# PSUM tiles from a pool in the unplanned part of a long-convolution decoder layer

## The chip, the cores and the metric

The kernel runs on one core of a Trainium2 chip. The metric is the device time of one execution in microseconds, as the median of several runs. A profile is one execution; its span runs from the first to the last instruction on the core, and the time of that execution is a little longer than its span.

## What is computed

One decoder layer with post-normalisation, on x of 4 x 1024 x 256 in float32:

```python
x = layernorm(x + longconv(x))         # projection to 3*256, depthwise conv of 3 taps,
                                       # two gated convolutions over all 1024 positions (by FFT)
x = layernorm(x + cross_attention(x, ctx))   # 16 heads, 64 context rows per batch
x = layernorm(x + ffn(x))              # gate/up/down of 1024, ternary weights, 8-bit activations
```

The filters of the two convolutions are themselves computed: `h = sin(10*(pe @ w1.T + b1)) @ w2.T + b2`, times a decay, plus a bias.

## The kernel before

The convolution is done with DFT matrices in place of an FFT. The channels are split into eight units: batch `b` (four) and half `dh` (two) of the 256 channels. Even and odd positions are kept apart, so that one transform of 1024 positions becomes small f32 matmuls against the tables `fw` (forward) and `gi_` (inverse).

Before the units comes the filter stage. `filter_basis` (L473) multiplies `pe` by `w1`, prepares the argument of the sine on VectorE, and lets ScalarE compute eight decay tiles (exponentials, into `q1_t`) and the sine. `stage_j(0)` issues the projections of unit 0 between the two halves of the filter work. `filters` (L489) then makes eight products with `w2` (`hp`), multiplies each by its decay on VectorE, and transforms the result with eight tiles of four `fw` matmuls each (`ha`); ScalarE copies one half of each `ha` tile out and VectorE forms sum and difference into `hf`.

Each unit goes through these stages:

- `stage_j` (L578): three projections of x (`project`, L533): four matmuls into one PSUM tile, which ScalarE reads four times: two halves into `xc` or `x1c`, and two shifted copies into `tap` tiles. GpSimd then issues two DMAs that add the taps onto `xc`, one after the other. There are two pairs of taps, so the third projection's taps wait until the first pair has been added.
- `stage_tv` and `stage_tx`: eight TensorE transposes of `xc` each, and one ScalarE copy into `vt` or `x0t`.
- `stage_f` (L599): the forward transform, 16 matmuls in two PSUM tiles; ScalarE copies a half, VectorE adds and subtracts.
- `stage_p` (L624): the product with the filter, on VectorE alone, into `q`.
- `stage_i0` (L669): the inverse transform, 16 matmuls into one PSUM tile. Parts 0, 1, 2 (12 matmuls) are issued ahead of the next unit's `stage_tv`, and part 3 behind it. `stage_i1` is the second convolution's inverse.
- `stage_o`: output projection, residual and layernorm.

The loop at L793 runs over units 0 to 6 and interleaves the stages of neighbouring units. Two things set the order. Up to unit 5 every call goes to the framework at once (line L61 in the profile); the framework's scheduler puts the instructions of an engine in order and may move one ahead of another where their data and their PSUM allow it. From unit 6 on (`if u == NU - 2`, L796) the calls are held back (`nc.hold`), the kernel's own planner (`plan`, L232) puts all held steps in order by estimated costs, and that order is pinned (line L82 in the profile, the call in `Engines.go`).

PSUM is one tile `ps_t` of 128 x 4096 f32, all eight banks (L412). A ring (`r_ps`) hands out four slots of 1024 columns, two banks each, strictly in turn. The framework tracks reads and writes of `ps_t` by bank. After the loop `space_of["rest"]` is set to the third slot, and the other slots go to attention and feed-forward (`big`, `small`).

Of the kernel before, what the change touches and what calls it, by code (L numbers as in the profile page):

```python
# [8 lines left out]
FP = mybir.dt.float32  # L9
# [5 lines left out]
PSUM = bass.MemoryType.PSUM  # L15

P = 128
# [266 lines left out]
def decoder_kernel(  # L284
# [63 lines left out]
    def split_biases():  # L348
        rest = spare[1][:, 0:6]
        nc.sync.dma_start(rest, rows.rearrange("r d -> (r d)").rearrange("(p c) -> p c", p=P))  # L350
        nc.gpsimd.memset(brow, 0.0)
        for q in range(3):
            part = spare[1][:, 8 + 8 * q : 16 + 8 * q].bitcast(BF)[:, 0:6]
            nc.vector.tensor_copy(part, rest)
            nc.sync.dma_start(
                brow[32 * q : 32 * q + 1].rearrange("o r d -> o (r d)").rearrange("o (p c) -> o p c", p=P), part
            )
            if q < 2:
                tt_(rest, rest, part, ALU.subtract)
# [49 lines left out]
    mw = const.tile([P, 3], FP, name="mw")  # L409
    rw = const.tile([P, 3], FP, name="rw")  # L410

    ps_t = ctx.enter_context(tc.tile_pool(name="ps", bufs=1, space=PSUM)).tile([P, 4096], FP, name="ps_t")  # L412
    r_ps = Ring(*(ps_t[:, 1024 * i : 1024 * i + 1024] for i in range(4)))
    space_of = {}

    def big1(name):
        return space_of["rest"] if space_of else r_ps()

    if True:
        taps = [tap_t[2 * i : 2 * i + 2] for i in range(NTAP)]  # L420
# [157 lines left out]
        def stage_j(u, *parts):  # L578

            b, dh = units[u]  # L580
            s = st_[u]
            for k in parts or range(3):
                name, ring, ct = (("vc", r_xc, 4), ("xc", r_xc, 0), ("x1", r_x1c, 2))[k]
                s[name] = ring()
                project(u, ct + dh, s[name])
                if k == 2 and dh == 1 and b + 1 < B:
                    load_x(b + 1)

        def stage_tv(u):
            s = st_[u]  # L590
            s["v"] = r_vt()
            turned(u, s["vc"], s["v"], "v")

        def stage_tx(u):
            s = st_[u]
            s["x0"] = r_x0t()
            turned(u, s["xc"], s["x0"], "x")

        def stage_f(u, n):  # L599

            s = st_[u]
            v = s["v"].rearrange("p (t d) -> p t d", t=8)
            vf = r_vf().rearrange("p (c s f) -> p c s f", c=2, s=2)
            s["vf"] = vf
            for cs in range(2):
                ps = big1(f"f{u}_{n}_{cs}")
                for par in range(2):
                    for kt in range(2):
                        o = par * 512 + kt * 256
                        m = (2 * cs + kt) * P  # L610
                        for mt in range(2):
                            mm(
                                ps[:, o : o + 256],
                                fw[:, 2 * par + mt, m : m + P],
                                v[:, 4 * par + 2 * mt : 4 * par + 2 * mt + 2, :],
                                start=mt == 0,
                                stop=mt == 1,
                            )
                vo = vo_t
                nc.scalar.copy(vo, ps[:, 512:1024])  # L620
                tt_(vf[:, cs, 0, :], ps[:, 0:512], vo, ALU.add)
                tt_(vf[:, cs, 1, :], ps[:, 0:512], vo, ALU.subtract)
# [46 lines left out]
        def stage_i0(u, *parts):  # L669

            s = st_[u]
            y = s["q", 0][1]
            if not parts or parts[0] == 0:
                s["i0"] = big1(f"i0_{u}")
            ps = s["i0"]
            for i in parts or range(4):
                par, mt = i // 2, i % 2
                o = i * 256
                for m in range(4):
                    mm(  # L680
                        ps[:, o : o + 256],
                        gi_[:, m, par * 256 + mt * P : par * 256 + mt * P + P],
                        y[:, par, m // 2, (m % 2) * 256 : (m % 2) * 256 + 256],
                        start=m == 0,
                        stop=m == 3,
                    )
            if not parts or parts[-1] == 3:
                s["v"] = r_vt()
                tt_(s["v"], ps, s["x0"], ALU.mult)

        def stage_i1(u):

            s = st_[u]
            b, dh = units[u]
            if dh == 0:
                v2s[b] = v2_t.rearrange("p (h l) -> p h l", h=2)
            y = s["q", 1][1]
            ps = big1(f"i1_{u}")
            for par in range(2):
                for j in range(2):  # L700
                    o = (2 * par + j) * 256
                    for m in range(4):
                        c = (m % 2) * 256 + j * P
                        mm(
                            ps[:, o : o + 256],
                            y[:, par, m // 2, c : c + P],
                            gi_[:, m, par * 256 : par * 256 + 256],
                            start=m == 0,
                            stop=m == 3,
                        )  # L710
            tt_(v2s[b][:, dh, :], ps, s["x1"], ALU.mult)

        def stage_o(b):

            for g in range(2):
                r = x1all[2 * b + g]
                nc.sync.dma_start(r, tokens(x, 2 * b + g))
                ps = big1(f"o{b}_{g}")
                for t in range(4):
                    c = (4 * g + t) * P  # L720
                    o = ps[:, t * D : t * D + D]
                    mm(o, ones16, brow[:, 0, :], start=True, stop=False)
                    for kt in range(2):
                        mm(o, v2s[b][:, kt, c : c + P], w_out_sb[:, kt, :], start=False, stop=kt == 1)
                rf = r.rearrange("p t d -> p (t d)")
                tt_(rf, ps, rf, ALU.add)
                layernorm(r, r, f"a{b}_{g}")
# [49 lines left out]
        def weights(u, place):  # L777
            for step, i in w_plan.get((u, place), ()):
                ternary(step, i)

        def move(i, dst):
            nc.sync.dma_start(dst, w_res[i])
# [10 lines left out]
        for u in range(NU - 1):  # L793
            if u == 1:
                split_biases()
            if u == NU - 2:  # L796

                nc.hold()
                nc.at = -40
            stage_p(u, 0, 0)  # L800
            weights(u, "p")
            nc.at += 1
            if u >= 2:
                stage_i1(u - 2)
            stage_p(u, 0, 1)
            nc.at += 1
            stage_j(u + 1, 0)
            nc.at += 1
            if u >= 1:
                stage_f(u - 1, 1)  # L810
            nc.at += 1
            stage_j(u + 1, 1, 2)
            nc.at += 1
            if u >= 1:
                stage_p(u - 1, 1, 0)
            nc.at += 1
            stage_i0(u, 0, 1, 2)
            weights(u, "i")
            nc.at += 1
            stage_tv(u + 1)  # L820
            nc.at += 1
            stage_i0(u, 3)
            weights(u, "t")
            nc.at += 1
            stage_f(u + 1, 0)
            nc.at += 1
            stage_tx(u + 1)
            nc.at += 1
            if u >= 1:
                stage_p(u - 1, 1, 1)  # L830
            nc.at += 1
            if u >= 2 and units[u - 2][1] == 1:
                stage_o(units[u - 2][0])

    u = NU - 1
    rest = [
        lambda: stage_p(u, 0, 0),
        lambda: stage_i1(u - 2),
        lambda: stage_p(u, 0, 1),
        lambda: stage_f(u - 1, 1),  # L840
        lambda: (move(0, hfree[1][:, 0:1024]), move(1, hfree[1][:, 1024:2048])),
        lambda: stage_p(u - 1, 1, 0),
        lambda: (stage_i0(u), stage_f(u, 1)),
        lambda: stage_p(u - 1, 1, 1),
# [14 lines left out]
    def small(name, dtype=FP):  # L859
        v = ps_t[:, 3072:3584] if name[0] in "akp" else ps_t[:, 3584:4096]  # L860
        return v if dtype == FP else v.bitcast(dtype)
# [32 lines left out]
    for dt in range(2):  # L894
        ps = small(f"k{dt}")
# [7 lines left out]
    for b in range(B):  # L903
        ps = small(f"v{b}")
# [272 lines left out]
                nc.at, nc.stage = i, "rest"  # L1177
                rest.pop(0)()

    space_of["rest"] = ps_t[:, 2048:3072]  # L1180
    nc.stage = "att_q"
    att_q(0)
    remains(2, 0)
    i, h = 0, 0
# [123 lines left out]
```

## Time and profile before

| | us |
|---|---|
| median of 3 runs | 764.66 (764.33 to 764.86) |
| the profiled execution | 765.34 |
| its span | 763.5 |
| TensorE matmuls busy | 710.0 (93%) |
| VectorE busy | 651.4 (85%) |
| ScalarE busy | 373.4 (49%) |
| GpSimd busy | 150.3 (20%) |
| mean granted TensorE clock | 0.974 of full |

How to read the rows: a row of the timeline starts with the start in us from the span's start, then the time it took, engine, source line, operation, output and inputs by the program's names, shapes, and the number of like instructions merged into it; in brackets stands the idle time of that engine before it and what ended it. PE is TensorE, DVE VectorE, ACT ScalarE, POOL GpSimd, SP SyncE. Tile numbers are left out of names, and all PSUM is `ps_t`. An f32 matmul makes two records and a transpose one. In the page, each digit of a line of 40 slices is a tenth of busy share, and PEclk is the TensorE clock that was granted. In rows by stretches of time the columns are the stretch, its length, busy time and number of instructions of PE, PE's weight loads, DVE, ACT and POOL, the granted clock, the busy share of the DMA engines and GB/s.

### The profile page before, as it was taken

What the parts mean: (1) busy time and instruction counts of PE and PEld (TensorE: products, weight loads), DVE (VectorE), ACT (ScalarE), POOL (GpSimd) and SP (SyncE); (2) the same over time, 40 slices, a digit from 0 to 9 for tenths busy, and PEclk for the clock granted to TensorE, in tenths of its full rate; (3) what the DMA queues carried; (4) which work ended last, traced back from release to release, by engine and by line L of the source; (5) the groups of instructions that cost most, each with busy time, mean ns of one, the idle gap of its engine ahead of it and who ended that gap; (6) DMA issues with size and microseconds to landing.
All of it is one profiled execution on the core that took longest, in us unless ns stands there. A gap on an engine that the chain in (4) does not pass through costs nothing. (4 is left out here: it accounts for less than half of the span.)

```text
span 763.5 us, 9645 instructions
## 1 busy us (share of the span) xinstructions
PE 710.0 (93%) x3606; PEld 511.0 (67%) x3606; DVE 651.4 (85%) x1189; ACT 373.4 (49%) x430; POOL 150.3 (20%) x214
## 2 busy tenths in 40 slices
PE   5899599999999999998999999999999999999863
PEld 1346286868687787876788787757676767767631
DVE  3446719999999999599979997989999999999984
ACT  2712516245361525224332213687778777868631
POOL 1210211111121112112000220122222322322322
PEclk9989989999999999999999999999999999999985
DMA  8572553537470644609601000012131322121232
GB/s 282 124 133 110 121 100 65 101 56 142 69 159 16 138 83 82 112 6 177 180 10 55 1 1 1 1 36 49 43 56 36 63 43 63 29 48 41 49 70 48
DMA packets 65140, 57.29 MB, mean 75 GB/s; under 512 B 38500, under 2 KB 49252, under 8 KB 65094
## 3 DMA queue, kind: packets, MB, share of 16 engines
q0 software_dynamic: 13056, 25.17, 19.3%
q1 hardware_dynamic: 47612, 27.84, 14.2%
q10 hardware_dynamic: 4426, 3.68, 1.7%
q8 instruction: 28, 0.46, 0.2%
q14 instruction: 18, 0.15, 0.1%
HBM read 17.34 MB, written 4.19 MB: 28 GB/s over the span
## 5 line engine op out<-in xcount | busy, mean ns | idle before, releaser
L82 PE MATMUL ps_t<-hf 128*128 128x512 bf16 (+1 forms) x512 | 100.3, 334 | 16.6 <-DMA hf<-vf 7.3
L82 PEld LDWEIGHTS <-hf 128*128 128x128 bf16 (+1 forms) x512 | 48.2, 100 | 57.7 <-issue 23.2
L61 PE MATMUL ps_t<-vt,fw 128*128 128x256 f32 x384 | 85.2, 380 | 0.9 <-ACT vt L61 0.6
L61 PEld LDWEIGHTS ps_t<-vt,fw 128*128 128x128 f32 x384 | 72.8, 190 | 13.5 <-issue 2.4
L61 PE MATMUL ps_t<-xt,w_in 128*128 128x512 f32 x168 | 76.4, 607 | 5.1 <-DMA w_in<-in_w_inT 5.1
L61 POOL DMA_DIRECT2D xc<-tap x28 | 33.9, 1245 | 207.1 <-ACT tap L61 133.5
L82 POOL TENSOR_TENSOR small_t<-small_t,mhalf 128x1 f32<-128x1 f32 x64 | 36.4, 574 | 157.6 <-DVE small_t L82 155.7
L82 PEld LDWEIGHTS ps_t<-hf,vt 128*128 128x128 f32 x512 | 61.0, 192 | 8.8 <-DVE small_t L82 3.1
L82 PE MATMUL ps_t<-hf,vt 128*128 128x34 f32 x512 | 61.9, 275 | 1.9 <-DVE xt L82 0.7
L61 PEld LDWEIGHTS ps_t<-xt,w_in 128*128 128x128 f32 x168 | 32.5, 195 | 43.1 <-issue 41.9
L61 ACT ACTIVATE tap<-ps_t,tbias,pv 128x1024 f32<-128x1024 f32 x42 | 48.6, 1210 | 11.4 <-DMA xc<-tap 11.4
L61 DVE TENSOR_TENSOR q<-q 128x1024 f32<-128x1024 f32 x44 | 53.0, 1218 | 0.4
L61 DVE TENSOR_TENSOR q<-vf,hf 128x1024 f32<-128x1024 f32 (+1 forms) x33 | 51.8, 1575 | 0.6
L61 ACT ACTIVATE xc<-ps_t,cbias,pv 128x512 f32<-128x512 f32 x28 | 21.5, 778 | 61.7 <-PE ps_t L61 61.7
L82 DVE SCALAR_TENSOR_TENSOR q<-ps_t,small_t,q 128x1024 f32<-128x1024 f32 x32 | 40.9, 1278 | 7.6 <-PE ps_t L82 4.6
L82 ACT ACTIVATE vf<-q,chalf,small_t 128x1024 f32<-128x1024 f32 x32 | 39.5, 1236 | 15.8 <-POOL small_t L82 8.1
L82 ACT ACTIVATE tap<-tap 128x1024 f32<-128x1024 f32 x32 | 33.8, 1056 | 25.6 <-DVE tap L82 25.4
L61 ACT COPY vo<-ps_t 128x512 f32<-128x512 f32 x24 | 14.0, 585 | 64.1 <-PE ps_t L61 47.4
L61 PE MATMUL ps_t<-q,gi__123 128*128 128x256 f32 x192 | 45.4, 393 | 0.0
L82 ACT ACT_TABLE_LOAD x34 | 43.6, 1283 | 2.2 <-PE ps_t L82 1.6
L82 ACT ACTIVATE q<-ps_t,small_t 128x1024 f32<-128x1024 f32 x32 | 35.6, 1113 | 17.5 <-PE ps_t L82 14.4
L61 DVE TENSOR_TENSOR vf<-ps_t,vo 128x512 f32<-128x512 f32 x48 | 31.1, 683 | 14.7 <-ACT vo L61 14.7
(149 smaller groups left out, 1493.4 us busy)
## 6 DMA issues: line engine op xcount, KB each, us to landing
xc<-tap POOLq DMA_DIRECT2D x32, 512.0 KB, 5.1
x1c<-tap POOLq DMA_DIRECT2D x16, 512.0 KB, 7.1
xt<-in_xT SPq DMA_DIRECT2D x8, 512.0 KB, 6.3
x1sp<-in_x SPq DMA_DIRECT2D x8, 512.0 KB, 4.6
out_y<-v SPq DMA_DIRECT2D x32, 128.0 KB, 1.7
hf<-x1sp SPq DMA_DIRECT2D x3, 512.0 KB, 2.9
fw<-in_dftf SPq DMA_DIRECT2D x1, 1024.0 KB, 14.0
gi__123<-in_dfti SPq DMA_DIRECT2D x1, 1024.0 KB, 10.7
```

What stands on the lines that cost most here:

```text
L61: return f(*a, **k)
L82: pin(steps[i].f(*steps[i].a, **steps[i].k))
```

## The change

The one PSUM tile of the whole kernel is split in time. Up to the planned part, each request for PSUM makes a tile of its own from a pool with four slots of 1024 columns; the framework assigns a slot that is free at that point of its schedule, and releases it when the last reader of that tile is done. Where the planned part begins the pool is closed, and a second pool is opened with one tile `ps_t` over all of PSUM; from there a ring of four slots serves as before, starting at its first slot. The function `big1` picks between the two. After the loop the third slot is wrapped in a ring of one, since `big1` now calls what it finds.

```diff
-    ps_t = ctx.enter_context(tc.tile_pool(name="ps", bufs=1, space=PSUM)).tile([P, 4096], FP, name="ps_t")
-    r_ps = Ring(*(ps_t[:, 1024 * i : 1024 * i + 1024] for i in range(4)))
+    psa = tc.tile_pool(name="psa", bufs=4, space=PSUM)
+    psa_p = psa.__enter__()
+
     space_of = {}
 
     def big1(name):
-        return space_of["rest"] if space_of else r_ps()
+        return space_of["rest"]() if space_of else psa_p.tile([P, 1024], FP, tag="big", name=name)
...
             if u == NU - 2:
 
+                psa.__exit__(None, None, None)
+                psb = ctx.enter_context(tc.tile_pool(name="psb", bufs=1, space=PSUM))
+                ps_t = psb.tile([P, 4096], FP, name="ps_t")
+                space_of["rest"] = Ring(*(ps_t[:, 1024 * i : 1024 * i + 1024] for i in range(4)))
                 nc.hold()
                 nc.at = -40
...
-    space_of["rest"] = ps_t[:, 2048:3072]
+    space_of["rest"] = Ring(ps_t[:, 2048:3072])
```

## The prediction

> **What bounds the kernel now.** I read the page's slices first, to see where TensorE is not full; then TensorE's and ScalarE's rows of the first 110 us in order of time; then the granted clock in 10 us stretches; then the place where the first pool closes.
>
> ```profile
> span 763.5 us, 9645 instructions
> ...
> PE   5899599999999999998999999999999999999863
> ...
>
> ```
>
> A slice is 19.1 us. TensorE is full except in slices 0, 1, 4 (76 to 95 us), 18 (344 to 363) and the end. From 107 us on it hardly waits: in 120 to 322 the waits view gives it 0.3 us in all, and in 366 to 480 0.7 us. So a microsecond won before 107 us moves everything after it. Rows of TensorE:
>
> ```profile
> 33.79 1.12 PE L61 MATMUL ps_t<-vf,x1sp 65*128 65x512 f32 x2
> 34.75 1.02 PE L61 MATMUL ps_t<-x1sp,fw 128*128 128x512 f32 x2
> 39.59 2.08 PE L61 MATMUL ps_t<-vf,x1sp 65*128 65x512 f32 x2 [3.82 <-ACT tap L61]
> 41.46 1.92 PE L61 MATMUL ps_t<-x1sp,fw 128*128 128x512 f32 x2
> 43.17 1.55 PE L61 MATMUL ps_t<-vf,x1sp 65*128 65x512 f32 x2
> ...
> 67.73 1.54 PE L61 MATMUL ps_t<-ident,xc 128*128 128x128 f32 x12
> 69.87 7.17 PE L61 MATMUL ps_t<-vt,fw 128*128 128x256 f32 x32 [0.60 <-ACT vt L61]
> 76.88 0.60 PE L61 MATMUL ps_t<-ident,xc 128*128 128x128 f32 x4
> 77.32 10.46 PE L61 MATMUL ps_t<-xt,w_in 128*128 128x512 f32 x24
> 96.19 1.94 PE L61 MATMUL ps_t<-ident,xc 128*128 128x128 f32 x8 [8.40 <-DMA xc<-tap]
> 97.92 9.22 PE L61 MATMUL ps_t<-q,gi__123 128*128 128x256 f32 x32
> ```
>
> Two stalls, 3.82 and 8.40 us, and slow matmuls behind each (an f32 matmul is two records, a transpose one). ScalarE's rows name the cause of the first:
>
> ```profile
> 16.24 0.78 ACT L61 ACTIVATE xc<-ps_t,cbias,pv 128x512 f32<-128x512 f32 x1 [8.83 <-PE ps_t L61]
> 16.92 4.99 ACT L61 ACTIVATE q<-vf,pv 128x512 f32<-128x512 f32 x8
> ...
> 38.33 1.21 ACT L61 ACTIVATE tap<-ps_t,tbias,pv 128x1024 f32<-128x1024 f32 x1 [4.60 <-DMA xc<-tap]
> ```
>
> A read of a projection stands ahead of eight exponentials that need no TensorE, so these, the table load and the sine run to 24.3, and the taps start only then. The last tap waits for an accumulating DMA and holds its PSUM slot to 39.54; ring order gives that slot to the seventh w2 product. Granted clock:
>
> ```profile
> 40.00:50.00 10.00, 10.00 (x19) 4.16 (x19) 5.34 (x8) 1.17 (x2) 2.40 (x2) 0.79 1.05 203
> 90.00:100.00 10.00, 3.81 (x13) 3.46 (x14) 2.02 (x2) 2.22 (x2) 3.45 (x3) 0.60 1.03 217
> ```
>
> [...] here the pair onto xc takes 5.0 and 7.4, so I use the trace's. [...]
>
> **Part 1, the filter stage.** The built order of the changed kernel differs. (a) ScalarE does exponentials, table load and sine before it reads the projection: from 7.4, 4.99 + 1.28, sine after VectorE's argument (14.57), done near 15.7. The first projection ends at 16.8, so its reads and taps end near 20.6 (27.1 before); the first accumulate goes out near 19.8 (26.35), the pair is home near 30, and the last tap is done near 31 (39.54). (b) Slots come free, not in turn: all eight w2 products go first, on whichever slot is free, then the 32 fw matmuls. None waits for the last tap before the third fw tile. TensorE's work is equal, 8 and 32.
>
> w2 products still start at 25.05, after the projections. The gate becomes VectorE: the second product waits for the first's read and ends at 27.87; the first fw tile waits for the read of the sixth, nine VectorE instructions on at about 0.69: 27.9 + 6.2 = 34.1. Thirty-two fw at (67.73 - 44.56)/27 = 0.858 take 27.5, so the transposes start at 61.7, not 67.73: -6.0, of which 3.6 is the stall less the new gaps and 2.4 the slow clock (39.59 to 44.56 for three matmuls worth 2.57). VectorE, then the end of ScalarE's vt copy, move along; the f stage starts at 63.8. Here four transposes of x no longer hide in the 0.60 wait but follow f: +0.44. Projections start at 71.7 and end at 82.2: -5.6.
>
> **Part 2, the first inverse transform.** Before, the v transposes, waiting for the accumulate until 96.19, stood ahead of all 16 inverse matmuls (97.92). In the changed order 12 of the 16 stand ahead of them, in a slot of their own. They need only VectorE's q: its last three rows start at 88.40 and end at 92.02, the second near 90.8; with -6.0 that is 84.8, a stall of 2.6 instead of 8.40. Warm, a stage of 16 takes 6.90 (322.95 to 329.85), so 12 take 5.2; a 2.71 us stall at 355 cost 1.8 extra (16 f matmuls in 8.70, not 6.90). I take it slow: done at 91.8. The accumulate, home at 96.05 before, moves by 5.6 to 90.4: hidden. Eight transposes 0.87, four inverse matmuls 1.73: f starts at 94.4 instead of 106.98: **-12.6**. Warm it would be -13.8.
>
> **Part 3, units 1 to 5.** A tile is now released whole, by its last reader, where a bank was before: TensorE's first write waits for ScalarE and VectorE together. Behind that wait stands all of TensorE. But a slot is reused some three tiles on, 3.4 to 7 us of TensorE work; ScalarE's waits in 120 to 322 show none on a DMA. Cost 0, at most 0.5 a unit. Nineteen more semaphore instructions on TensorE's queue: matmul spacing around the present ones (0.21 or 0.43) is undisturbed; 0, at most 1 in all.
>
> **Part 4, where the pool closes.** The new tile covers all of PSUM, so its first writer waits for the last readers of the old pool.
>
> ```profile
> 322.08 1.03 PE L61 MATMUL ps_t<-w_out_sb,v 128*128 128x256 f32 x4
> 322.95 7.07 PE L82 MATMUL ps_t<-gi__123,q 128*128 128x256 f32 x32
> ...
> 324.84 1.22 DVE L61 TENSOR_TENSOR x1sp<-ps_t,x1sp 128x1024 f32<-128x1024 f32 x1
> ...
> 357.71 8.86 PE L82 MATMUL ps_t<-vt,fw 128*128 128x256 f32 x32 [2.71 <-ACT vt L82]
> ```
>
> The planned inverse transform would start at 326.1, not 322.95: 3.2 us, and about 1.8 of slow clock: +5.0. VectorE isn't behind it: it reads that result at 337.81, ready at 335.0. Then comes the 2.71 us stall at 355 with its 1.8: 4.5 us of cover. The vt copy moves only with ScalarE's queue (projection reads about +1.6, and context loads issued behind them), and the second xc1 accumulate, home at 366.08 for the transposes at 366.41, moves as much. I take +1.2 of the 5.0; bounds -0.5 and 5.0. The plan's early order moves a few key projections and transposes by about a microsecond with no wait: 0. From there on the order is that of before.
>
> **Sum.** -12.6 + 1.2 = -11.4. The profiled execution is 765.34 us, 763.5 of it span: 753.9. The median shown is 764.66, 0.7 lower, so **753.3 us**.
>
> **Rivals.** *B, the pool's close is paid in full:* if ScalarE's reads and the DMA pair also slip by the whole 5.0, -12.6 + 5.0 gives 757.1. For: the pair ahead of 366 has only 0.3 us to spare. Against: it is issued behind VectorE-bound work.
> *C, the first accumulates don't come home earlier:* they run at a DMA share of 1.03 beside the x load. If the v transposes still start at 96.1, f starts at 96.1 + 0.87 + 1.73 = 98.7: -8.3 + 1.2 gives 757.6.
> *D, slower:* whole-tile release puts the second tap of a projection in TensorE's way in every unit. Price: one blocked tap, 6.25 us in the trace (before 96.13), of which some 3 would show. It decides from 11.4/6 = 1.9 us a unit; at 3.0 the time is 764.7 - 11.4 + 18 = 771. Against: in the unit at 114.76 taps end at 121.4, some 5 us before the slot is wanted.
> *E, no change:* the order differs, but something at a fixed time takes the gain back. No load in 107 to 340 is such a bound; 764.7.
>
> **How the numbers follow.** Forecast 0.64 (its own range 750.8 to 756), B 0.15, C 0.11, D 0.06, E 0.04. Low end: -13.8 and a close at zero. High end: C with 1.4 of other waits. 750.5 to 759 leaves out D, E and a little. A difference of 0.2% (1.5 us) is about what a measurement of this kernel can tell. Faster 0.90, same 0.04, slower 0.06.
>
> **What would show it.** The transposes of unit 0 near 61.7; ScalarE's eight exponentials before its first projection read; 12 inverse matmuls ahead of the v transposes of unit 1 and f near 94; no TensorE wait over 0.5 us between there and 310; a TensorE wait of some 3 us on VectorE's x1sp near 313 and less than 1 us where 2.71 stood. A wait on a tap in each unit, or v transposes of unit 1 held past 95 by the DMA, would prove me wrong.

## The result, and the profile after

| | before | after |
|---|---|---|
| median, first measurement | 764.50 us (764.01 to 764.86, 4 runs) | 754.53 us (752.98 to 759.92, 4 runs) |
| ratio after/before, 95% interval | | 0.9883 (0.9833 to 0.9932) |
| the profiled execution, and its span | 765.34, 763.5 | 752.98, 751.2 |
| TensorE matmuls busy | 710.0 | 705.3 |
| mean granted TensorE clock | 0.974 | 0.986 |

The kernel is 1.2% faster; 753.3 us was forecast for the median. Two further measurements of the changed kernel on other chips gave 0.9867 (0.984 to 0.9895) and 0.9872 (0.9841 to 0.9903). By the medians measured beside each other the gain was 10.0, 9.4 and 11.2 us; 11.4 was forecast. The single times of the changed kernel lie further apart (752.98 to 759.92 us) than the first four of before did. The kernel before scatters as widely when it is measured more often (761.3 to 770.1 us in 27 runs), so this is no effect of the change; what it consists of comes under the first experiment.

First the page of the changed kernel: its span and TensorE's line of 40 slices.

```profile
span 751.2 us, 9662 instructions
...
PE   5999899999999999899999999999999999999862
```

Between the first slice and the last three, all are full but two: 75 to 94 us and 300 to 319 us, an 8 each. Next TensorE's rows in order of time. The PSUM tiles have names of their own now: `trv` of the v transposes, `pj` of projections, `i` of the inverse, `o` of the output projection.

```profile
61.61 1.04 PE L61 MATMUL trv<-ident,xc 128*128 128x128 f32 x8
...
71.63 10.47 PE L61 MATMUL pj<-xt,w_in 128*128 128x512 f32 x24
84.81 7.03 PE L61 MATMUL i<-q,gi__122 128*128 128x256 f32 x24 [2.72 <-DVE q L61]
91.69 1.04 PE L61 MATMUL trv<-ident,xc 128*128 128x128 f32 x8
```

Compared with the starts of before, in brackets, the v transposes of unit 0 are at 61.61 (67.73) and the projections at 71.63 (77.32). The stall of 8.40 us on `xc<-tap` is gone; 12 inverse matmuls start at 84.81 after 2.72 us on VectorE's q, and the v transposes come behind them without a wait. f of unit 1 follows at 94.29, where before it was:

```profile
106.98 7.07 PE L61 MATMUL ps_t<-vt,fw 128*128 128x256 f32 x32
```

ScalarE's rows show why the filter stage is shorter:

```profile
7.53 5.01 ACT L61 ACTIVATE q<-vf,pv 128x512 f32<-128x512 f32 x8
...
33.52 1.21 ACT L61 ACTIVATE tap<-pj,tbias,pv 128x1024 f32<-128x1024 f32 x1 [5.36 <-DMA xc<-tap]
```

The exponentials run at 7.53 instead of 16.92, ahead of the first projection read, which now comes at 18.36 with its taps right behind it. The last tap is done at 34.73 instead of 39.54. The stretch that had a clock of 0.60 before:

```profile
90.00:100.00 10.00, 10.00 (x52) 8.87 (x51) 2.63 (x4) 2.81 (x3) 2.40 (x2) 1.00 0.97 168
```

It is full and at full clock, and so is the one from 40 to 50 us, which had 0.79. Last, the place where the pool closes, TensorE and VectorE:

```profile
313.18 8.83 PE L82 MATMUL ps_t<-gi__122,q 128*128 128x256 f32 x32 [3.10 <-DVE x1sp L61]
...
346.83 7.07 PE L82 MATMUL ps_t<-vt,fw 128*128 128x256 f32 x32
353.74 1.04 PE L82 MATMUL ps_t<-ident,xc 128*128 128x128 f32 x8
```

```profile
311.82 1.22 DVE L61 TENSOR_TENSOR x1sp<-o,x1sp 128x1024 f32<-128x1024 f32 x1
```

The first planned inverse waits 3.10 us for VectorE's residual add, and its 16 matmuls take 8.83 instead of 7.07 (the clock from 310 to 320 us is 0.83). But f at 346.83 has no wait, where before 2.71 us stood with 8.86 behind it. The x transposes of unit 7 come next, at 353.74; before they stood here:

```profile
366.41 1.04 PE L82 MATMUL ps_t<-ident,xc 128*128 128x128 f32 x8
```

The stretch from the end of the output projection to these transposes is 43.46 us before (322.95 to 366.41). In the changed kernel the last group of the output projection starts at 309.05; before, the next group came 0.87 after such a start (322.08 to 322.95), which puts its end at 309.92 and makes the stretch 43.82 us. The difference of 0.36 is that of the two waits, each with what its matmuls lost: 3.10 + 1.76 in place of 2.71 + 1.79.

### The profile page after: what moved, and what is told of

Same layout as the page of the kernel before. It is cut to its first block, busy times and chain, and to the rows that moved or that the text cites. A ratio compares the mean times of both kernels' runs of the same rounds, so it can differ in the third digit from the quotient of the medians.

```text
span 751.2 us, 9662 instructions
## 1 busy us (share of the span) xinstructions
PE 705.3 (94%) x3606; PEld 508.9 (68%) x3606; DVE 650.5 (87%) x1189; ACT 372.7 (50%) x430; POOL 151.1 (20%) x214
## 5 line engine op out<-in xcount | busy, mean ns | idle before, releaser
L61 PE MATMUL f<-vt,fw 128*128 128x256 f32 x384 | 84.9, 379 | 1.1 <-ACT vt L61 1.1
L61 PEld LDWEIGHTS f<-vt,fw 128*128 128x128 f32 x384 | 72.9, 190 | 13.3 <-issue 2.4
L61 PE MATMUL pj<-xt,w_in 128*128 128x512 f32 x168 | 75.8, 604 | 5.7 <-DMA w_in<-in_w_inT 5.7
L61 PEld LDWEIGHTS pj<-xt,w_in 128*128 128x128 f32 x168 | 32.3, 194 | 43.3 <-issue 42.6
L61 ACT ACTIVATE tap<-pj,tbias,pv 128x1024 f32<-128x1024 f32 x42 | 48.8, 1218 | 11.4 <-DMA xc<-tap 11.3
L61 ACT ACTIVATE xc<-pj,cbias,pv 128x512 f32<-128x512 f32 x28 | 20.3, 777 | 59.3 <-PE pj L61 59.3
L61 PE MATMUL i<-q,gi__122 128*128 128x256 f32 x192 | 45.1, 390 | 2.7 <-DVE q L61 2.7
L82 ACT ACTIVATE tap<-tap 128x1024 f32<-128x1024 f32 x32 | 33.8, 1056 | 26.9 <-DVE tap L82 26.8
L61 PEld LDWEIGHTS i<-q,gi__122 128*128 128x128 f32 x192 | 37.1, 196 | 10.7 <-DVE q L61 3.5
L61 DVE TENSOR_TENSOR vf<-f,vo 128x512 f32<-128x512 f32 x48 | 31.1, 683 | 14.4 <-ACT vo L61 14.4
```

Of the source, the lines that this page charges most:

```text
L61: return f(*a, **k)
L82: pin(steps[i].f(*steps[i].a, **steps[i].k))
```

## The experiments

In what follows the transposes at 353.74 of the changed kernel are x transposes of unit 7; those at 344.23 are its v transposes. Where an expectation speaks of v transposes of unit 7 at 353.7, the former are meant.

Theory: the change works through the order of instructions in two early places, and its close puts one wait in the place of another. Rivals: that it needs slots handed out of turn; that the close costs several microseconds which a better version would save.

### The changed kernel again

> The changed kernel once more, to see how far its four times (752.98 to 759.92 us, the kernel before 764.01 to 764.86) are its own. Theory 'the gain is 12.4 us and the rest is scatter': the profiled execution again has unit 0's v transposes at 61.6, f of unit 1 at 94.3, the 3.1 us wait at 313 and f of the planned part at 346.8, each within 0.3 us, and the median lies 11 to 12.5 us below before. Rival 'the new order is sensitive to when the transfers come home': one of these places moves by more than 1 us, and the long executions are long there.

> The changed kernel a third time, beside the three above. Median 754.5 to 757, with a spread of some 6 us. v transposes of unit 0, f of unit 1 and the wait at the close as before (61.6 to 63, 94.3 to 96, 3.1 us); what differs between its executions are stretches of lowered clock behind waits under 1 us.

Measured, in this order: 756.66 us (753.92 to 759.50, 6 runs) and 754.82 (754.22 to 760.39, 6 runs), the kernel before beside them 766.02 (11 runs, 762.83 to 769.79) and 766.0 (27 runs, 761.3 to 770.1). The two profiled executions took 759.50 and 754.22. The first lies 9.4 us below before, less than the 11 to 12.5 set down. In its profiled execution everything from the w2 products on is 1.2 us late, since the projections end later (26.25 instead of 25.02), and f of unit 1 starts at 95.62. So the rival is right that places move by more than 1 us, but the larger part of the long execution's extra time is not there. From the output projection to the x transposes of unit 7 it takes 43.83 us, in the second 43.82: that stretch repeats to 0.01 us. Behind it the three executions differ most: from those transposes to the end of the span 397.5, 402.1 and 398.9 us. The granted clock in a 5 us stretch shows one reason, first in the execution of 752.98 us, then in that of 759.50:

```profile
440.00:445.00 5.00, 5.00 (x27) 4.15 (x26) 4.41 (x22) 0.36 (x1) 0.56 (x1) 1.00 0.00 0
```

```profile
440.00:445.00 5.00, 4.89 (x24) 4.27 (x25) 5.00 (x19) 1.06 (x1) 1.95 (x3) 0.69 0.00 0
```

Both have the same wait of 0.71 us on VectorE ahead of the same matmul (438.29 and 440.11). In one the clock stays at 1.00, in the other it falls to 0.69. From the x transposes of unit 7 to one later group of transposes (717.41 in the first execution) it takes 363.67, 366.95 and 362.08 us. In stretches of 10 us, the first has one place with a lowered clock there (670, at 0.83), the second three (440, 630 and 680, at 0.83, 0.85 and 0.83) and the third none up to 710: about 1.6 us for each. The remaining 33.8, 35.2 and 36.8 us, the end of the kernel, differ by slow matmuls (in stretches of 10 us the clock falls to 0.50, 0.51 and 0.50) and by waits on transfers into `hf` (the longest 3.9 us in the first and 4.9 in the second). Why the clock falls behind a wait in one execution and not in the next is not shown.

### The order alone, with the PSUM of before

```diff
+        def pin_if(on, instruction):
+            if on and instruction is not None:
+                tc.keep_in_program_order(instruction)
...
-            act(efd, fdb[:, 0, :], AF.Exp)
+            pin_if(1, act(efd, fdb[:, 0, :], AF.Exp))
...
-                    mm(
+                    pin_if(u == 0 and i < 3, mm(
...
-                        nc.tensor.transpose(ps[:, o : o + P], src[:, c : c + P], ident)
+                        pin_if(name == "v" and u == 1, nc.tensor.transpose(ps[:, o : o + P], src[:, c : c + P], ident))
```

The eight exponentials, the sine, and the two reads of each of unit 0's projections into `xc` or `x1c` are pinned in the same way; the `mm` shown is that of `stage_i0`.

> PSUM as in the kernel before, one tile and a ring, no pool and no close; only the order of two places is pinned: ScalarE does the eight exponentials and the sine ahead of unit 0's projection reads, and 12 inverse matmuls of unit 0 stand ahead of the v transposes of unit 1. Theory 'the change acts through the order alone': v transposes of unit 0 at 61.5 to 62.5 (before 67.73), f of unit 1 at 94 to 95 (before 106.98), no wait at 310, the 2.7 us wait ahead of f of the planned part is back, f there at 346 to 348 as in the changed kernel (346.83), and the time is that of the changed kernel within 1 us, 752 to 754 in the profiled execution. Rival 'slots that come free out of turn are needed too': a tap still holds the seventh w2 product or the inverse matmuls, and the time is 757 to 761. Rival 'the pool's close costs something after all': the order is as good and, with no close, f of the planned part comes 1 to 5 us earlier than 346.83, 748 to 752 in all.

Measured on the chip of the first repeat: 756.52 us (754.49 to 758.56), ratio 0.9872 (0.9846 to 0.9898); the changed kernel there 756.66. The profiled execution took 754.81, 0.8 us above what was set down. TensorE's rows:

```profile
61.63 1.54 PE L61 MATMUL ps_t<-ident,xc 128*128 128x128 f32 x12
...
84.89 7.11 PE L61 MATMUL ps_t<-q,gi__123 128*128 128x256 f32 x24 [3.20 <-issue]
...
345.29 10.17 PE L82 MATMUL ps_t<-vt,fw 128*128 128x256 f32 x32 [2.81 <-ACT vt L82]
```

There is no pool and no close, the seventh w2 product still stands behind fw matmuls as in the kernel before, and the places are those of the changed kernel: 61.63, and f of unit 1 at 94.43. So the gain comes from the order in two places; slots handed out of turn are not needed. The wait of 3.20 us at 84.89, for which the view names no releaser, I take for the same wait for q: in the changed kernel VectorE's last three rows of it start at 82.27 and the inverse matmuls at 84.81. The planned inverse starts at 310.43 without a wait, and the wait on ScalarE's vt copy is back, 2.81 us. f at 345.29 is 1.5 us ahead of the changed kernel's, where the third outcome has it; but it runs slow, 10.17 for 7.07 (clock 0.56 from 344 to 349 us and 0.76 from 349 to 354), and the x transposes behind it come at 355.30, 1.6 us later than there. So nothing is won without the close, and the time is not the 748 to 752 of that outcome.

One place at a time, with the same edits:

> PSUM as before, and only the second of the two places pinned: 12 inverse matmuls of unit 0 ahead of the v transposes of unit 1. By the prediction's parts this is 12.6 less the 5.6 of the filter stage: f of unit 1 at about 100 instead of 106.98, time 757 to 758.5. The accumulate is home at 96.05 there, so the inverse matmuls hide it fully: with the 12 matmuls from 90.4 to 97.3. If the two parts are not additive (the accumulate shared by both sets the end): less than 5 us, 760 or more.

> PSUM as before, and only the first place pinned: ScalarE's exponentials and sine ahead of its projection reads. Theory: v transposes of unit 0 at 61.5 to 62.5 instead of 67.73, and since VectorE's q and the accumulate both move along by some 5.6, all of it is kept: f of unit 1 at 101 to 102, time 758.5 to 760. Rival 'ring order keeps the stall': the seventh w2 product still waits over 2 us for the last tap, 762 or more. Rival 'the accumulate does not come earlier': v transposes of unit 1 stay at 96, 764.

Measured: 759.74 (756.95 to 763.14), ratio 0.9913 (0.9884 to 0.9942) with the inverse matmuls alone, and 762.00 (760.55 to 762.79), ratio 0.9942 (0.9921 to 0.9963) with ScalarE's order alone. TensorE's rows, the first kernel and then the second:

```profile
91.30 5.42 PE L61 MATMUL ps_t<-q,gi__123 128*128 128x256 f32 x24 [3.20 <-issue]
97.07 1.06 PE L61 MATMUL ps_t<-ident,xc 128*128 128x128 f32 x8 [0.35 <-DMA xc<-tap]
```

```profile
90.92 1.94 PE L61 MATMUL ps_t<-ident,xc 128*128 128x128 f32 x8 [8.89 <-DMA xc<-tap]
```

f of unit 1 starts at 99.70 in one, 7.28 us earlier than before, and at 101.03 in the other, 5.95 earlier; both together gave 12.55. So the two parts nearly add up. With the inverse matmuls first the wait on the accumulate shrinks to 0.35; the median is 1.2 us above the 757 to 758.5 set down. With ScalarE's order alone the accumulate is home 5.27 us earlier (90.92 for 96.19), and TensorE still waits 8.89 us for it; the v transposes of unit 0 are at 61.97, so the mechanism of neither rival is seen. At the end it is worth 4.0 us by the medians, less than at f: 762.0 is 2 us above what was set down, and is the time that the first rival named, though without its stall. The kernel before was itself 1.5 above its first median on this chip. The interval, 2.8 to 6.1 us, takes in the 5.95; in the profiled execution 6.0 us are still kept at the x transposes of unit 7 (360.37 for 366.41), so the rest is lost behind them.

### What the close costs

The pool closed a stage earlier, ahead of the output projection; the same lines at `if u == NU - 2` are taken out:

```diff
+            if u == NU - 3:
+                psa.__exit__(None, None, None)
+                psb = ctx.enter_context(tc.tile_pool(name="psb", bufs=1, space=PSUM))
...
             if u >= 2 and units[u - 2][1] == 1:
                 stage_o(units[u - 2][0])
```

> The changed kernel with the pool closed a stage earlier, ahead of the output projection of the fifth and sixth units' batch instead of behind it. The last reader of the old pool is then VectorE's work on f, not the residual add, so the wait at the close falls from 3.1 us to about 1 to 2 us and moves to about 301. Theory 'the close is covered': the planned inverse starts 1 to 3 us earlier than 313.2, the wait on ScalarE's vt copy ahead of f comes back by as much, and the v transposes of unit 7 stay within 1.5 us of 353.7; time unchanged within 1.5 us. Rival 'the close is paid': all places from 313 on move up by 1.5 to 4 us and so does the time, a median near 752.

Measured: 757.13 us (754.72 to 763.27), ratio 0.9896 (0.9861 to 0.9932): no faster than the changed kernel. The wait at the close is 1.17 us:

```profile
304.09 0.28 PE L61 MATMUL ps_t<-brow,ones 128*128 128x256 bf16 x1 [1.17 <-DVE vf L61]
...
346.85 7.17 PE L82 MATMUL ps_t<-vt,fw 128*128 128x256 f32 x32 [2.89 <-ACT vt L82]
355.35 1.06 PE L82 MATMUL ps_t<-ident,xc 128*128 128x128 f32 x8 [1.32 <-DMA xc<-tap]
```

The planned inverse starts at 311.90, 1.28 us earlier than at 313.18, though this execution was 0.64 us later ahead of the close, and it runs at full clock (7.07; 1.00 from 310 to 320 us). All of that is given back: 2.89 us on the vt copy and 1.32 on the accumulate. The x transposes of unit 7 are at 355.35, not earlier than 353.74.

Then the loads that stand between ScalarE's instructions were put on SyncE's queue, in the changed kernel, in the ring kernel with both places pinned, and in the kernel before:

```diff
-        pin(nc.scalar.dma_start(dst, src))
+        pin(nc.sync.dma_start(dst, src))
```

> The changed kernel, with the context and attention weight loads that stand between ScalarE's instructions of the planned part issued from SyncE's queue instead. Theory 'the close of the pool is paid for by a stall that would have come anyway, ScalarE's late vt copy behind those loads': with that cover gone the close still holds the planned inverse at 313 for 3.1 us with slow matmuls behind it, so the v transposes of unit 7 stay within 1 us of the 353.7 of the changed kernel and the time within 1.5 us of it (a median of 753 to 757). Rival 'the loads have nothing to do with it': the same numbers here, so its twin without a pool decides.

> The kernel with one PSUM tile, ring and the two pinned places (no pool, no close), with the same loads issued from SyncE's queue. Theory: no wait at 310, and the 2.8 us wait on ScalarE's vt copy ahead of f of the planned part (345.29) shrinks below 1 us; f at 341.5 to 343.5, and the v transposes behind it at 349 to 353.5, where the accumulate for them is the next to be late. The time is 2 to 5 us below its twin with the pool: that is the close's price without cover. Rival 'the vt copy is late for another reason': the 2.8 us wait stays, and the time is that of the ring kernel with ordinary loads (756.5 median, 754.8 profiled).

> The kernel before with nothing changed but the queue of the loads (SyncE's instead of ScalarE's). In the kernel before 2.71 us of wait on ScalarE's vt copy stand at 355, with f at 8.86 instead of 7.07 behind it. If the loads cause that wait, it shrinks or turns into a wait of the v transposes on their accumulate, with the matmuls behind it at full speed: 0 to 3 us below before. If the 3 to 4 us that the ring kernel gained by this edit were scatter, there is no difference.

> The ring kernel with the two pinned places and moved loads once more, on the same chip as the changed kernel below: 752.9 was its median, and 751.19 to 754.18 its times. If that was its own and not the chip's, the median is again 752 to 754, and 2 to 4 us below the changed kernel's. Its 2.8 us wait ahead of the v transposes at 342.6 was followed by matmuls at full speed; where the same wait finds the clock drop, 1.8 to 3.3 us go.

| kernel, loads on SyncE | median (runs) | ratio to before | wait in the stretch | output projection to x transposes of unit 7 |
|---|---|---|---|---|
| changed | 756.61 (753.88 to 759.89) | 0.9880 (0.9848 to 0.9912) | 3.10, close | 44.09 |
| ring, both pinned | 752.90 (751.19 to 754.18) | 0.9832 (0.9805 to 0.9858) | 2.79, accumulate | 41.78 |
| the same again | 752.50 (752.01 to 754.37) | 0.9826 (0.9801 to 0.9851) | 2.32, accumulate | 41.31 |
| before | 765.67 (761.34 to 768.97) | 0.9997 (0.9980 to 1.0014) | 3.01, accumulate | 43.69 |

Rows of TensorE, the pinned ring kernel first, then the kernel before, both with moved loads:

```profile
342.57 1.07 PE L82 MATMUL ps_t<-ident,xc 128*128 128x128 f32 x8 [2.79 <-DMA xc<-tap]
...
345.21 7.07 PE L82 MATMUL ps_t<-vt,fw 128*128 128x256 f32 x32
```

```profile
354.47 1.07 PE L82 MATMUL ps_t<-ident,xc 128*128 128x128 f32 x8 [3.01 <-DMA xc<-tap]
355.37 3.25 PE L82 MATMUL ps_t<-q,gi__123 128*128 128x256 f32 x8
```

My reading of the cover fell in one point. Moving the loads does take the wait on the vt copy away, but a wait of nearly the same length stands on the accumulate for the v transposes instead, and f is no earlier (345.21 for 345.29). The move itself brings this wait, because the loads run earlier and not only from another queue. In the ring kernel with the loads on ScalarE the first of them is issued at 339.36, and in the two stretches of 1.35 us from 333.65 on the DMA engines move 0 and 38 GB/s; with the loads on SyncE they move 364 and 199 in the same two. The stretch from 330 to 340 us, with the loads on ScalarE and then on SyncE:

```profile
330.00:340.00 10.00, 10.00 (x38) 6.70 (x38) 9.90 (x10) 5.66 (x8) 2.40 (x2) 1.00 0.67 116
```

```profile
330.00:340.00 10.00, 9.79 (x35) 6.27 (x33) 9.90 (x11) 5.74 (x8) 2.40 (x2) 1.00 0.97 221
```

With the loads on ScalarE the v transposes start at 339.72 without a wait for the accumulate; with the loads on SyncE they wait for it until 342.57, beside busier DMA engines (0.97 for 0.67). So these runs do not tell what the stretch would take if no load stood in it at all.

In every one of these kernels this stretch holds between 2.3 and 4.2 us of waits (the early close's 1.17 apart), at the close, at the vt copy or at the accumulate. With the loads on ScalarE the close costs 0.36 us against the kernel before, and neither its removal nor an earlier close gains anything. With the loads on SyncE the kernel without a close is 3.7 us faster by the medians (the intervals of the two ratios just overlap). That is what its expectation had for a close without cover, 2 to 5 us, though f did not come earlier as it should have. In the profiled executions the stretch is 2.3 and 2.8 us shorter without the close, and 1.76 of this is the slow inverse behind the close. The 3.1 us by which the moved loads shorten the stretch in the ring kernel (44.87 to 41.78) are clock: f takes 7.07 there and 10.17 with the loads on ScalarE (from 340 to 350 us the clock is 1.00 and 0.73). In the kernel before the same move ends in a lower clock behind its wait (3.25 us for eight matmul records that take 1.89; clock 0.83 from 350 to 360 us), and gains nothing. That was set down as the sign that the ring kernel's gain is scatter; its repetition at 752.50 speaks against this. Why the pinned ring kernel with moved loads kept the full clock there in both profiled executions (1.00 from 340 to 350 us) stays open, and with it how much of the difference is the close's own price. The profiled execution of the first row also lost some 5 us in the filter stage, where 35 to 40 us had a clock of 0.50.

### Filling the two waits that are left

In the ring kernel with both places pinned, unit 0's third projection is moved into the wait for q, and its x transposes into the wait for the vt copy:

```diff
-        stage_j(0)
+        stage_j(0, 0, 1)
         filters()
         stage_tv(0)
-        stage_f(0, 0)
         stage_tx(0)
+        stage_f(0, 0)
...
-            stage_j(u + 1, 1, 2)
+            stage_j(u + 1, 1)
+            if u == 0:
+                stage_j(0, 2)
+            stage_j(u + 1, 2)
```

> The ring kernel with the two pinned places, and two further moves of order: unit 0's third projection (x1, needed only by the second convolution) is issued with the projections of unit 1 instead of ahead of the filter stage, and unit 0's x transposes ahead of its f. Theory 'the 2.7 us wait for q and the 1.1 us wait for the vt copy are idle time of TensorE that other work can fill': the w2 products start 3.4 us earlier, v transposes of unit 0 near 58.2, the inverse matmuls start near 82 with a wait under 0.7 us, f of unit 1 near 90 instead of 94.4, and the time is 3.5 to 5 us below the ring kernel's, a median of 751.5 to 753. Rival 'the taps and accumulates come next': the later third projection holds its PSUM slot and the taps' tiles, v transposes or f of unit 1 wait for a transfer, and less than 2 us are won.

Measured: 758.65 us (756.44 to 763.82), ratio 0.9920 (0.9890 to 0.9951): by the ratios slower than the ring kernel with the same loads (0.9872, on another chip), and f of unit 1 is 2.4 us later (96.85 for 94.43). TensorE, then ScalarE:

```profile
96.85 0.79 PE L61 MATMUL ps_t<-vt,fw 128*128 128x256 f32 x1 [9.33 <-ACT vt L61]
```

```profile
94.69 1.21 ACT L61 ACTIVATE tap<-ps_t,tbias,pv 128x1024 f32<-128x1024 f32 x1 [4.15 <-DMA xc<-tap]
95.80 1.00 ACT L61 COPY vt<-ps_t 128x1024 f32<-128x1024 f32 x1
```

The wait for q was filled, as the theory says: the inverse matmuls start at 79.50 after 0.21 us. But one projection more now has to share two pairs of tap tiles, and ScalarE stands at three taps until a transfer is home (4.42, 3.93 and 4.15 us), with the vt copy queued behind. The rival was right. A third pair of tap tiles, in columns of `x1sp` that are free between the filter stage and the weight loads, takes that away; loads on SyncE as above, and the two moves of order kept:

```diff
+        flat = x1sp.rearrange("p g c -> p (g c)")
+        third = [flat[:, o : o + L + 2] for o in (6 * L - 4, 7 * L - 2)]
...
-            pair = taps[npad[0] % NTAP]
-            npad[0] += 1
+            if u == 1 and ct != 1:
+                pair = third
+            else:
+                pair = taps[npad[0] % NTAP]
+                npad[0] += 1
```

> The ring kernel with the two pinned places, loads on SyncE's queue, unit 0's third projection late and unit 0's x transposes early, and now a third pair of tap tiles in a part of x1sp that is free then, for the first and the third projection of unit 1. Theory 'ScalarE's three blocked taps were what held the vt copy to 95.8': no tap waits for a transfer there, f of unit 1 starts at 87 to 89, some 6 to 7 us ahead of the ring kernel's 94.3, and the median lies 5 to 7 us below the 752.9 of the ring kernel with moved loads: 746 to 748.5. Rival 'the x load of the next batch or VectorE, busy 98% from 100 to 200, is the next bound': f of unit 1 comes as early, but TensorE waits again between 94 and 130, and less than 3 us are kept.

Measured: **748.62 us** (747.80 to 749.78), ratio 0.9772 (0.9748 to 0.9796); on the same chip the changed kernel 754.82 and the pinned ring kernel with moved loads 752.50. It beats both kernels, the latter by 3.9 us: more than the 3 that its rival allowed, less than the 5 to 7 set down. TensorE's rows:

```profile
87.02 7.07 PE L61 MATMUL ps_t<-vt,fw 128*128 128x256 f32 x32
...
336.68 1.90 PE L82 MATMUL ps_t<-ident,xc 128*128 128x128 f32 x8 [3.15 <-DMA xc<-tap]
```

f of unit 1 is 7.3 us ahead of the changed kernel's, and of the taps ahead of it one waits, 1.15 us, for a transfer; the vt copy waits for none. Between there and the output projection only one wait came back, 1.42 us at 95.52 on the accumulate for the x transposes. The planned inverse starts at 304.07, 6.7 us ahead of the 310.77 of the pinned ring kernel's second execution; the x transposes of unit 7 at 347.89 are 4.2 ahead (352.08). The other 2.5 went at 336.68: 0.8 in a longer wait and 1.7 in the slow matmuls behind it (clock 0.84 from 330 to 340 us).

## Why the prediction was right, point by point

**Part 1, filter stage.** Right: transposes at 61.61 (61.7 forecast; its own terms, 34.1 + 27.5, make 61.6), f at 63.75 (63.8), projections 71.63 (71.7). Of its two causes only (a), ScalarE's order, was needed: with slots in turn and w2 products between fw matmuls the transposes stand at 61.63 and 61.97. In (a) the last tap was done at 34.73, not near 31. The first accumulate went out at 21.22, not 19.8, and the last tap started 12.3 us behind it; before it was 12.0 (26.35 to 38.33), where the forecast left some 10. This mis-sized term did no harm: the w2 products have all started by 34.14, so none waits for the slot.

**Part 2, first inverse transform.** Right, in each step: start 84.81 (84.8), slow, done 91.69 (91.8), f at 94.29 (94.4): -12.69 for -12.6. The choice of slow matmuls for this wait rested on one earlier instance. It held in all three executions of the changed kernel, but not in the kernel with the inverse order alone, where 3.20 us of wait cost no clock (5.42 us; 1.00 from 90 to 100 us). So the wait was worked out, and its 1.8 us of lower clock (0.83 from 80 to 90 us) was in part luck.

**Part 3, whole-tile release and semaphores.** Right: from f of unit 1 to the end of the output projection 215.63 us, against 215.97 before and 216.00 in the ring kernel with the same order. The waits view shows no TensorE wait from 95 to 310 us.

**Part 4, the close.** The mechanism held: 3.10 us on VectorE's x1sp (3.2) and 1.76 of slow clock (1.8), and no wait where 2.71 stood. The net was mis-sized: +1.2 was taken, +0.36 measured (43.82 for 43.46), inside the bounds of -0.5 and 5.0. I had let the vt copy move with ScalarE's queue and kept a part of its wait; nothing of the wait was left. Rival B, the full 5.0, is refuted by the +0.36; rival C by the v transposes at 91.69, which do not wait for the accumulate; D by the missing waits from 95 to 310, and E by the time.

**Sum.** At the x transposes of unit 7 the gain is 12.67 us in place of 11.4, and 12.36 at the end of the profiled execution, 752.98 for 753.9. The profiled execution was the fastest of the four, so the closeness of its total is in part luck; that of its places is not. The median of the four runs lies 1.2 us above the forecast, as the other executions took 0.9 to 6.9 us longer. The one long execution that was profiled (759.50) shows 6.5 us of this: 1.8 by the x transposes of unit 7, of which 1.2 ahead of the w2 products, and 4.7 behind them, of which about 3.3 with lowered clock in two places more. The prediction set 1.5 us as what a measurement of this kernel can tell and had no term for such differences; the 27 runs of the kernel before spread over 8.8 us.

## What to carry to other kernels

A pool in place of a ring changed the time ahead of its close only through the order that the framework's scheduler chose with it (f of unit 1 at 94.29 with it, 94.43 with the order alone); look for the two or three instructions that changed places, pin them in the old kernel, and see whether the pool is needed at all. A wait that appears where another disappears cost only the difference here (0.36 us), so find every wait of the stretch and what is late behind it before pricing a new one. Work moved into a gap takes its buffers with it: the third projection filled TensorE's wait, and TensorE then stood 9.33 us behind tap tiles until there was a third pair.

## What the runs showed of the hardware

In these runs the cost of a TensorE wait was not fixed by its length. Each row gives the time that the matmuls behind a wait took above the time that the same matmuls take elsewhere at full clock:

| wait, us | loss behind it, us | kernel, place |
|---|---|---|
| 0.71 | 0 and 1.7 | changed, two executions, matmuls behind 440 (22 records in 5.00 and 6.68 us) |
| 2.32, 2.79 | 0, 0 | ring pinned with moved loads, v transposes of unit 7 |
| 2.66, 2.71, 2.72 | 1.7, 1.8, 1.8 | ScalarE's order alone; before; late third projection; f near 350 |
| 2.78, 2.89 | 0.1, 0.1 | inverse order alone; early close; f near 350 |
| 2.81 | 3.1 | ring pinned, f at 345.29 |
| 2.72 | 1.6 to 1.8, four executions | changed, with and without moved loads; inverse matmuls at 84.8 |
| 3.01, 3.15 | 1.7, 1.7 | before and third pair, loads moved; v transposes of unit 7 |
| 3.10 | 1.76, in each of four executions | the close |
| 3.20 | 1.6 to 1.8, three executions, and 0.1 | ring pinned, and inverse order alone; inverse matmuls |

For these waits of 2.3 to 3.2 us the losses lie near 0, near 1.7 or at 3.1. Behind the longest waits, those of unit 1, they differ as much: 3.0 us behind 8.40 (before), 1.5 behind 8.66 (before, loads moved), 2.3 behind 8.89 (ScalarE's order alone) and 2.3 behind 9.33 (late third projection). And some 5.1 us went in the filter stage of the changed kernel with moved loads, behind waits of 0.78, 0.20 and 0.20 us. The longer wait was not always the dearer one: 2.89 us cost 0.1 and 0.71 us cost 1.7.

The waits of 2.66 to 2.72 us, seven in this table, each cost 1.6 to 1.8; one of 0.71 cost 1.7 in one execution, with a granted clock of 0.69 from 440 to 445 us, and nothing in another. So a wait of well under 1 us was not safe here. What decides whether the clock falls behind a wait, and why the most frequent loss is near 1.7 us, was not shown.
